# Three sums of softplus: from GpSimd and VectorE instructions to accumulating transfers

## The chip, the cores and the metric

The kernel runs on one core of a Trainium2 chip. The core has five engines with a queue each: PE (TensorE, matrix products), DVE (VectorE), ACT (ScalarE), POOL (GpSimd) and SP (SyncE, which here issues transfers). Sixteen DMA engines move data. Each queue runs in order; queues wait for each other through semaphores. The metric is the device time of one execution in microseconds.

## What is computed

The reference is a two-layer network on images of 8 x 128 x 128 x 96. Layer 0 is a convolution in the frequency domain with a small quantized feed-forward part. Layer 1 is a selective scan in two directions, again with a feed-forward part. The change lies in the step sizes of the scan:

```python
delta = jax.nn.softplus(dts + dt_projs_bias.reshape(1, Kk, DIi, 1))
...
def step(h, inp):
    u, dlt, Bt, Ct = inp
    dA = jnp.exp(dlt[..., None] * As)
    h = dA * h + (dlt * u)[..., None] * Bt[:, :, None, :]
    y = jnp.sum(h * Ct[:, :, None, :], axis=-1)
    return (h, y)
```

The kernel computes softplus(x) as max(x, 0) + log(1 + e), with e = exp(-|x|). Adding 1 to a small e loses low bits, so a correction is kept: with w = 1 + e as rounded, the lost part is (w - 1) - e, and the result is log(w) - ((w - 1) - e) + max(x, 0).

## The kernel before

**Tiles.** `scan_layer` treats two images at a time (four rounds) in chunks of 1,024 tokens: 16 chunks forward (d = 0), then 16 backward (d = 1), 128 in all. The 192 channels of two images make three tiles of 128 rows. A chunk has 12 blocks of 32 channels of one image; a block has 4 units, each with 4 of the 16 states on 128 rows. So a chunk has 48 units, and a unit is one scan.

**A block.** PE spreads `du` (delta times u) over the states (`dub`, `spread`). DVE multiplies it with `bt` for two units at once (`inject`, L1298, 128x2048). ACT makes the decay `da` = exp(delta A) for each unit (`decay`, L1281), with two buffers in PSUM. DVE scans (`scan`, L1333); ACT keeps the last column (`keep`, L1342); POOL multiplies with `ct` (`read`, `hc`, L1349); PE sums over the states (`total`, `y`, L1358). In some blocks of forward chunks (the numbers in `SHARE`) ACT copies `dub` to the SBUF tile `dus` (`fetch`, L1310), and POOL makes the product of the block's last unit (`inject_shared`, L1317), so that DVE's second `inject` has half its size.

**Preparation.** While a chunk is scanned, `prepare_steps` makes delta and `du` of the next one, for three tiles in the order 0, 2, 1. For each: PE's `delta` (`pd`, two halves), ACT's `parts` (|x| into `e`, max(x, 0) into `rl`), ACT's `exp`, `onep` (w = 1 + e) and `log`, DVE's `lost`, POOL's `sub` and `add`, SP's store of w to DRAM (`dld`, from which the scan loads `dlb`), and POOL's `mul` with u (`du`). The tiles `e`, `rl`, `w`, `dus` have one buffer each.

**Beside it.** Forward chunks also carry the depthwise convolution for later chunks (`conv_steps`): nine products on PE for each half tile (`taps`, `pv`, L1081), an eviction on ACT (`evict`, L1095), and after both halves a silu with two loads of ACT's function tables (`silu`, L1106 and L1107). Backward chunks carry output projection and feed-forward part (`finish_steps`) and six gates on POOL (L1414). `pv`, `pd`, `px`, `po` and the feed-forward products share one PSUM buffer, the tag `pp`.

**Order.** It is written out by hand. Every step is given to `plan` with a position in units, and `Plan.emit` issues all steps sorted by it; within an engine that is the order of execution. `PREP` holds the positions of the preparation (relative to the start of the chunk that is being scanned), `SLOTS` those of the convolution: taps from 3.2, 16.2, 26.2, 31.1, 39.1 and 43.6 on, an eviction 4.4 later, the silu 5 after the second.

Of the kernel before, what the change touches and what calls it, by code (L numbers as in the profile page):

```python
# [9 lines left out]
F32 = mybir.dt.float32  # L10
# [3 lines left out]
AF = mybir.ActivationFunctionType  # L14
ALU = mybir.AluOpType
# [14 lines left out]
TC = 1024  # L30
# [911 lines left out]
def scan_layer(tc, p, x2d, xcd, zsd, ud, yfd, dld, bcd, out):  # L942
# [7 lines left out]
    nc = tc.nc  # L950
# [3 lines left out]
    with ExitStack() as ctx:  # L954
# [28 lines left out]
        w1 = ctx.enter_context(tc.tile_pool(name="sc1", bufs=1))  # L983
# [64 lines left out]
        def halves():  # L1048
            return [(i, slice(i * HALF, (i + 1) * HALF)) for i in range(2)]

        def kind(t):
            return 0 if t < 2 else 1
# [74 lines left out]
        def prepare_steps(plan, bp, d, c, k, at0):  # L1127


            k.u, k.du = [None] * 3, [None] * 3  # L1130

            def load(t):
                k.u[t] = w1.tile([128, TC], F32, tag=f"u{t}", name="u")
                nc.sync.dma_start(k.u[t], ud[bp % 2, t, :, c * TC : (c + 1) * TC])

            def project(i, hs):
                def f():
                    if i == 0:
                        k.bc = w1.tile([NX, TC], F32, tag="bc", name="bc")
                    px = ps1.tile([NX, HALF], F32, tag="pp", name="px")  # L1140
                    for t in range(3):
                        nc.tensor.matmul(  # L1142
                            px, xpw[:, d, t, :], k.u[t][:, hs], start=(t == 0), stop=(t == 2)
                        )
                    k.px = px

                return f

            def projected(hs):
                nc.scalar.copy(k.bc[:, hs], k.px)  # L1150

            def store_bc():
                nc.sync.dma_start(bcd[k.s], k.bc[0 : 4 * NST])


            def delta(t, st, i, hs):
                def f():
                    if i == 0:
                        st["e"] = w1.tile([128, TC], F32, tag="e", name="e")
                        st["r"] = w1.tile([128, TC], F32, tag="rl", name="rl")  # L1160
                    pd = ps1.tile([128, HALF], F32, tag="pp", name="pd")
                    nc.tensor.matmul(  # L1162
                        pd, dtw[4 * NST : NX, d, t, :], k.bc[4 * NST : NX, hs], start=True, stop=True
                    )
                    st["pd"] = pd

                return f

            def parts(t, st, hs):
                bias = dtb[:, d, kind(t) : kind(t) + 1]  # L1170
                nc.scalar.activation(st["e"][:, hs], st["pd"], AF.Abs, bias=bias)  # L1171
                nc.scalar.activation(st["r"][:, hs], st["pd"], AF.Relu, bias=bias)  # L1172

            def exp(st):
                nc.scalar.activation(st["e"], st["e"], AF.Exp, scale=-1.0)

            def onep(st):
                st["w"] = w1.tile([128, TC], F32, tag="w", name="w")
                nc.scalar.activation(st["w"], st["e"], AF.Copy, bias=1.0)

            def log(st):
                nc.scalar.activation(st["w"], st["w"], AF.Ln)  # L1182

            def lost(st):
                nc.vector.scalar_tensor_tensor(  # L1185
                    st["e"], st["w"], -1.0, st["e"], ALU.add, ALU.subtract
                )

            def sub(st):
                nc.gpsimd.tensor_tensor(st["w"], st["w"], st["e"], ALU.subtract)  # L1190

            def add(st):
                nc.gpsimd.tensor_tensor(st["w"], st["w"], st["r"], ALU.add)  # L1193

            def store(t, st):
                nc.sync.dma_start(dld[k.s, t], st["w"])

            def mul(t, st):
                k.du[t] = w1.tile([128, TC], F32, tag=f"du{t}", name="du")
                nc.gpsimd.tensor_tensor(k.du[t], st["w"], k.u[t], ALU.mult)  # L1200

            for t, at in ((0, 0.4), (1, 3.2), (2, 4.2)):
                plan(at0 + at, lambda t=t: load(t))
            for i, hs in halves():
                plan(at0 + 9.2 + 1.3 * i, project(i, hs))
                plan(at0 + 10.2 + 1.1 * i, lambda hs=hs: projected(hs))
            plan(at0 + 12, store_bc)
            for t, at in ((0, PREP[0]), (2, PREP[1]), (1, PREP[2])):
                st = {}
                for i, hs in halves():  # L1210
                    plan(at0 + at["delta"][i], delta(t, st, i, hs))
                    plan(at0 + at["delta"][i] + 0.6, lambda t=t, st=st, hs=hs: parts(t, st, hs))
                for what, f in (
                    ("exp", exp), ("onep", onep), ("lost", lost), ("log", log), ("sub", sub),
                    ("add", add),
                ):
                    plan(at0 + at[what], lambda f=f, st=st: f(st))
                plan(at0 + at["mul"], lambda t=t, st=st: mul(t, st))
                plan(at0 + at["store"], lambda t=t, st=st: store(t, st))
# [248 lines left out]
        def finish_steps(plan, bp, c, prs, i, at0, x2_at, at):  # L1468
# [172 lines left out]
            for t, f in zip(at, steps, strict=True):  # L1641
# [7 lines left out]

        PREP = tuple(  # L1650
            {
                "delta": (a0, a1), "exp": e, "onep": e + 0.2, "lost": e + 1.5, "log": e + 2.2,
                "sub": s0, "add": s1, "mul": m, "store": s1 + 1.1,
            }
            for a0, a1, e, s0, s1, m in (
                (12.2, 13.2, 16.2, 20.3, 21.3, 24.3),
                (24.2, 25.2, 28.2, 32.3, 33.3, 36.3),
                (37.2, 38.2, 41.2, 45.3, 48.3, 49.3),
            )
        )  # L1660

        SLOTS = ((3.2, 16.2), (26.2, 31.1), (39.1, 43.6))
# [11 lines left out]
            return [tuple(UN * (n - a) + x for x in s) for a, s in zip(ahead, slots)]  # L1674


        SHARE = (1, 2, 3, 4, 7, 10)
        GATE = (9.9, 17.9, 25.9, 37.3, 41.9, 50.5)

        FINISH = (  # L1680
# [17 lines left out]
        with tc.manual_schedule():  # L1698
            plan = Plan()
            plan(-300, lambda: nc.vector.memset(h0, 0.0))  # L1700
            plan(UN * -2 + 20, prepare_constants)
            plan(UN * -2 + 37, scan_constants)
            for bp in range(B // 2):
                first = len(jobs) * bp
                if bp > 0:
                    plan(UN * (first - 8), lambda: nc.vector.memset(h0[:, 0], 0.0))
                    plan(UN * (first + 8), lambda: nc.vector.memset(h0[:, 1], 0.0))
                for n, (d, c) in enumerate(jobs):
                    k = Params()
                    k.s = n % 4  # L1710
                    at0 = UN * (first + n)
                    share = SHARE if d == 0 and (bp == 0 or n > 0) else ()
                    prs = scan_steps(plan, bp, d, c, k, at0, share)
                    if d == 1:
                        for b2 in range(2):
                            for i in range(2):
                                finish_steps(
                                    plan, bp, c, prs[3 * b2 : 3 * b2 + 3], i, at0, *FINISH[b2][i]
                                )
                    prepare_steps(plan, bp, d, c, k, at0 - UN)  # L1720
                    if d == 0:
                        conv_steps(plan, bp, c, conv_slots(bp, n))
            plan.emit()


@with_exitstack
def kernel(ctx: ExitStack, tc: tile.TileContext, p: Params, out: bass.AP):
    nc = tc.nc
    dp = ctx.enter_context(tc.tile_pool(name="scratch", bufs=1, space=DRAM))
    tall = dp.tile([96, M, 2 * KW], F32, name="tall")  # L1730
    x2d = dp.tile([B, H, W, C + 1], F32, name="x2d")
    xcd = dp.tile([B, M, XROWS, W], F32, name="xcd")
    zsd = dp.tile([B, M, L], F32, name="zsd")
    ud = dp.tile([2, 3, 128, L], F32, name="ud")
    yfd = dp.tile([6, 128, L // 2], F32, name="yfd")
    dld = dp.tile([4, 3, 128, TC], F32, name="dld")
    bcd = dp.tile([4, 4 * NST, TC], F32, name="bcd")

    layer0(tc, p, tall, x2d, xcd, zsd)
    scan_layer(tc, p, x2d, xcd, zsd, ud, yfd, dld, bcd, out)  # L1740
# [109 lines left out]
```

## Time and profile before

| | us |
|---|---|
| median of 3 runs | 26,206.75 (26,201.54 to 26,208.22) |
| profiled execution | 26,211.62 |
| its span, first to last instruction | 26,209.8 |
| DVE busy | 25,009.4 (95%) |
| POOL busy | 22,513.3 (86%) |
| PE busy | 22,077.0 (84%) |
| ACT busy | 17,596.9 (67%) |
| DMA, mean busy share of 16 engines | 41.7% (queue of SP's transfers) |

The profile lists instructions in groups: line, engine, operation, output <- inputs, count, then busy time and the mean length of one, then the idle time of the engine just before them and what ended it. A timeline row gives the start, the length, engine, line and operation of an instruction, or of several of a kind merged (x3), and in brackets the idle time before it. `PEld` is PE's loading of weights, `SPq` the queue of SP's transfers. Layer 0 takes the first 5,100 us or so; the first scan starts at 5,167.47 us, and the 128 chunks follow. The first forward chunks take about 160 us and the first backward ones about 167.

### The profile page before, as it was taken

Reading aid. Unit: us, or ns where it says so; the run is one execution under the profiler, and the core shown is the slowest. Engines: PE = TensorE matmul, PEld = TensorE weight load, DVE = VectorE, ACT = ScalarE, POOL = GpSimd, SP = SyncE. Lnnn points to the kernel's source line nnn. Section 1 sums busy time; section 2 is a strip of 40 time slices with the busy share of each in tenths; the row PEclk is TensorE's granted clock in tenths of the full one; section 3 lists DMA queues with packets and bytes.
Section 4 is the critical chain, followed back from the end, with each engine's and each line's share of the span. In section 5 each row is a group of like instructions: output and inputs, shape, how many; then the busy total and the mean of one; then the engine's idle time right before and its main releaser. Section 6 shows DMA issues by size and latency. Waiting matters only on the chain.

```text
span 26209.8 us, 272243 instructions
## 1 busy us (share of the span) xinstructions
PE 22077.0 (84%) x84560; PEld 8860.1 (34%) x84560; DVE 25009.4 (95%) x18513; ACT 17596.9 (67%) x31774; POOL 22513.3 (86%) x13817
## 2 busy tenths in 40 slices
PE   9999999899997777889877778889777788977777
PEld 7777777522222222222222222222222222212222
DVE  7888888699999999999999999999999999999999
ACT  7888777566666666666666666666666666656666
POOL 5666666499999999999999999999999999999998
PEclk9999999999998888999988889999888899988888
DMA  3333333344444444444444434444444444444443
GB/s 88 93 93 91 90 89 87 106 156 155 153 156 135 138 139 133 156 155 153 154 138 140 136 134 154 157 154 153 139 138 134 138 151 157 156 139 138 136 136 115
DMA packets 1887106, 3513.56 MB, mean 134 GB/s; under 512 B 564382, under 2 KB 999190, under 8 KB 1885626
## 3 DMA queue, kind: packets, MB, share of 16 engines
q1 hardware_dynamic: 1885652, 3496.14, 41.7%
q8 instruction: 672, 11.01, 0.2%
q14 instruction: 782, 6.41, 0.1%
HBM read 2739.32 MB, written 756.17 MB: 133 GB/s over the span
## 4 chain that ended last, share of the span: by engine, by line
DVE 41%; PE 17%; issue 16%; ACT 5%; POOL 3%; DMA 0%; DVEq 0%; POOLq 0%; SPq 0%; ACTq 0%
DVE hp L1333 22%; DVE hp L1298 17%; PE pv L1081 6%; PE y L1358 5%; PE dub L1268 4%; POOL hc L1349 2%; DVE e L1185 2%; ACT da L1281 2%; PE po L1492 1%; PE y L1400 1%; PE px L1142 1%; ACT ff_h L1589 0%; ACT ln_q L1519 0%; PE pd L1162 0%; ACT pre L1095 0%
## 5 line engine op out<-in xcount | busy, mean ns | idle before, releaser
L1349 POOL TENSOR_TENSOR hc<-hp,ct 128x1024 f32<-128x1024 f32 x6144 | 14726.6, 2416 | 1162.7 <-DVE hp L1333 1085.3
L1333 DVE TENSOR_TENSOR_SCAN hp<-da,h,hp 128x1024 f32<-128x1024 f32 x6144 | 14142.8, 2337 | 200.2 <-ACT da L1281 39.6
L1358 PE MATMUL y<-hc,sely 128*32 128x512 f32 x24576 | 6906.9, 646 | 2163.5 <-POOL hc L1349 2145.6
L1281 ACT ACTIVATE da<-dlb,at 128x1024 f32<-128x1024 f32 x6144 | 6845.0, 1114 | 1.1 <-ACT h L1342 1.1
L1298 DVE TENSOR_TENSOR hp<-bt,dub 128x2048 f32<-128x2048 f32 (+1 forms) x3072 | 6551.7, 2133 | 12.7 <-PE dub L1268 12.4
L1268 PE MATMUL dub<-du,selx 128*128 128x512 f32 x6144 | 3686.2, 731 | 1385.5 <-DVE hp L1298 1385.3
L1342 ACT COPY h<-hp 128x1 f32<-128x1 f32 x6144 | 1159.3, 189 | 4831.1 <-DVE hp L1333 4814.5
L1081 PE MATMUL pv<-xin,cdiag 128*128 128x512 f32 x6912 | 3489.9, 624 | 94.2 <-ACT pre L1095 55.1
L1358 PEld LDWEIGHTS y<-hc,sely 128*32 128x32 f32 x24576 | 931.7, 111 | 6682.7 <-POOL hc L1349 4523.0
L1268 PEld LDWEIGHTS dub<-du,selx 128*128 128x128 f32 x6144 | 1237.8, 217 | 3458.5 <-issue 2129.3
L1081 PEld LDWEIGHTS pv<-xin,cdiag 128*128 128x128 f32 x6912 | 1171.9, 190 | 2438.5 <-issue 2035.3
L110 POOL TENSOR_SCALAR ln_v<-ln_v 128x4 f32<-128x4 f32 x768 | 198.7, 259 | 1179.3 <-DVE ln_v L106 1159.2
L1317 POOL TENSOR_TENSOR hp<-bt,dus 128x1024 f32<-128x1024 f32 x366 | 867.2, 2369 | 254.5 <-ACT dus L1310 208.1
L1095 ACT ACTIVATE pre<-pv,cbt 128x512 f32<-128x512 f32 x384 | 263.8, 687 | 1076.4 <-PE pv L1081 889.9
L1190 POOL TENSOR_TENSOR w<-w,e 128x1024 f32<-128x1024 f32 x384 | 903.4, 2353 | 52.0 <-ACT w L1182 38.6
L1162 PE MATMUL pd<-bc,dtw 12*128 12x512 f32 x1536 | 887.5, 658 | 71.7 <-ACT rl L1172 49.3
L111 POOL TENSOR_TENSOR ln_r<-ln_v,mhalf 128x4 f32<-128x4 f32 x768 | 887.1, 1155 | 64.0
L1200 POOL TENSOR_TENSOR du<-w,u 128x1024 f32<-128x1024 f32 x384 | 907.4, 2363 | 0.2
L1193 POOL TENSOR_TENSOR w<-w,rl 128x1024 f32<-128x1024 f32 x384 | 905.3, 2357 | 0.2
L1171 ACT ACTIVATE e<-pd,dtb 128x512 f32<-128x512 f32 x768 | 524.8, 683 | 499.7 <-PE pd L1162 484.6
L770 PE MATMUL ring<-xnt,win 96*128 96x512 f32 x1536 | 778.5, 615 | 69.1 <-ACT xnt L764 68.1
L1142 PE MATMUL px<-u,xpw 128*76 128x512 f32 x1536 | 716.5, 602 | 80.5 <-ACT ff_h L1582 78.3
(189 smaller groups left out, 32830.3 us busy)
## 6 DMA issues: line engine op xcount, KB each, us to landing
dlb<-dld SPq DMA_DIRECT2D x1536, 512.0 KB, 5.3
bt<-bcd SPq DMA_DIRECT2D x1024, 512.0 KB, 5.0
ct<-bcd SPq DMA_DIRECT2D x1024, 512.0 KB, 4.5
u<-ud SPq DMA_DIRECT2D x384, 512.0 KB, 5.0
dld<-w SPq DMA_DIRECT2D x384, 512.0 KB, 3.5
ud<-pre SPq DMA_DIRECT2D x192, 512.0 KB, 3.6
yf<-ud SPq DMA_DIRECT2D x768, 128.0 KB, 4.8
yfd<-yo SPq DMA_DIRECT2D x384, 256.0 KB, 6.5
```

What stands on the lines that cost most here:

```text
L1081: nc.tensor.matmul(st["pv"], cdiag[:, kind(t), j, :], st["xin"][:, r : r + HB // 2, j % 3 : j % 3 + W], start=(j == 0), stop=(j == 8),)
L1142: nc.tensor.matmul(px, xpw[:, d, t, :], k.u[t][:, hs], start=(t == 0), stop=(t == 2))
L1190: nc.gpsimd.tensor_tensor(st["w"], st["w"], st["e"], ALU.subtract)
L1193: nc.gpsimd.tensor_tensor(st["w"], st["w"], st["r"], ALU.add)
L1200: nc.gpsimd.tensor_tensor(k.du[t], st["w"], k.u[t], ALU.mult)
L1268: nc.tensor.matmul(blk["du"][:, hs], selx[:, blk["r"], :], k.du[blk["t"]][:, hs], start=True, stop=True,)
L1281: nc.scalar.activation(un["da"], blk["dl"], AF.Exp, scale=at[:, d, blk["kb"], j : j + 1])
L1298: nc.vector.tensor_tensor(hp[:, 0:n, :], bt[blk["b2"], j][:, 0:n, :], blk["du"].rearrange("p (o t) -> p o t", o=1).to_broadcast([128, n, TC]),
L1333: nc.vector.tensor_tensor_scan(h, da, h, un["init"], op0=ALU.mult, op1=ALU.add)
L1342: nc.scalar.copy(un["init"], un["h"][:, last : last + 1])
L1349: nc.gpsimd.tensor_tensor(un["hc"], un["h"], ct[blk["b2"], j], ALU.mult)
L1358: nc.tensor.matmul(y[q, :], sely, un["hc"][:, hs], start=False, stop=(j == NG - 1),)
```

## The change

`lost` leaves DVE and `sub` and `add` leave POOL's arithmetic. All three become transfers that POOL issues and that add one SBUF tile to another. For that ACT makes m = 1 - w in a new step (`minus`), in the buffer of `dus`. `sub` follows `lost` and `add` by three to four units, the store and `mul` follow `sub` by about three. `add` and `sub` change places. The first tile's `delta` comes a little earlier, the second's a little later. The blocks with shared products are others; their number stays.

```diff
+            def minus(st):
+                st["m"] = w1.tile([128, TC], F32, tag="dus", name="m")
+                nc.scalar.activation(st["m"], st["w"], AF.Copy, scale=-1.0, bias=1.0)
+
             def log(st):
                 nc.scalar.activation(st["w"], st["w"], AF.Ln)
 
+
             def lost(st):
-                nc.vector.scalar_tensor_tensor(
-                    st["e"], st["w"], -1.0, st["e"], ALU.add, ALU.subtract
-                )
+                nc.gpsimd.dma_start(st["e"], st["m"], accum_op=ALU.add)
+
+            def add(st):
+                nc.gpsimd.dma_start(st["w"], st["r"], accum_op=ALU.add)
 
             def sub(st):
-                nc.gpsimd.tensor_tensor(st["w"], st["w"], st["e"], ALU.subtract)
-
-            def add(st):
-                nc.gpsimd.tensor_tensor(st["w"], st["w"], st["r"], ALU.add)
+                nc.gpsimd.dma_start(st["w"], st["e"], accum_op=ALU.add)
...
-                    ("exp", exp), ("onep", onep), ("lost", lost), ("log", log), ("sub", sub),
-                    ("add", add),
+                    ("exp", exp), ("onep", onep), ("minus", minus), ("log", log), ("lost", lost),
+                    ("add", add), ("sub", sub),
...
-                "delta": (a0, a1), "exp": e, "onep": e + 0.2, "lost": e + 1.5, "log": e + 2.2,
-                "sub": s0, "add": s1, "mul": m, "store": s1 + 1.1,
+                "delta": (a, a + 1), "exp": e, "onep": e + 0.2, "minus": e + 1, "log": e + 1.2,
+                "lost": e + 2.1, "add": e + 3.1, "sub": s, "mul": s + 3, "store": s + 2.9,
             }
-            for a0, a1, e, s0, s1, m in (
-                (12.2, 13.2, 16.2, 20.3, 21.3, 24.3),
-                (24.2, 25.2, 28.2, 32.3, 33.3, 36.3),
-                (37.2, 38.2, 41.2, 45.3, 48.3, 49.3),
-            )
+            for a, e, s in ((11.6, 16.2, 22.3), (24.4, 28.2, 34.3), (37.2, 41.2, 47.3))
...
-        SHARE = (1, 2, 3, 4, 7, 10)
+        SHARE = (0, 1, 2, 3, 6, 9)
```

## The prediction, made before the result was known

> **What bounds it now.** I read the busy times first, then the groups of instructions, then DVE's, PE's and ACT's timelines side by side for one chunk. The groups (operation, count, busy us, mean ns, idle before):
>
> ```profile
> L1349 POOL TENSOR_TENSOR hc<-hp,ct 128x1024 f32<-128x1024 f32 x6144 | 14726.6, 2416 | 1162.7 <-DVE hp L1333 1085.3
> L1333 DVE TENSOR_TENSOR_SCAN hp<-da,h,hp 128x1024 f32<-128x1024 f32 x6144 | 14142.8, 2337 | 200.2 <-ACT da L1281 39.6
> ...
> L1185 DVE SCALAR_TENSOR_TENSOR e<-w,e 128x1024 f32<-128x1024 f32 x384 | 535.4, 1394 | 80.7 <-ACT w L1179 80.7
> ```
>
> DVE sets the end: from 8,000 to 11,000 us it is busy 2,971.71 us (99%), POOL 2,789.03 (93%). The 384 corrections of softplus lie in DVE's queue and are 2% of the span. But a forward chunk has a second limit. One of its blocks on DVE (start, length):
>
> ```profile
> 6394.18 2.25 DVE L1298 TENSOR_TENSOR hp<-bt,dub 128x2048 f32<-128x2048 f32 x1
> ...
> 6407.73 2.26 DVE L1298 TENSOR_TENSOR hp<-bt,dub 128x2048 f32<-128x2048 f32 x1
> ...
> 6414.53 6.93 DVE L1333 TENSOR_TENSOR_SCAN hp<-da,h,hp 128x1024 f32<-128x1024 f32 x3
> ```
>
> A plain block takes 13.55 us (6,394.18 to 6,407.73). A block with a shared product takes 12.48 (1.07 less), one correction adds 1.13 to 1.4. PE in the same stretch, from the spread for block 7 to the last convolution tap before block 9, and ACT after it:
>
> ```profile
> 6374.03 3.49 PE L1268 MATMUL dub<-du,selx 128*128 128x512 f32 x4 [1.66 <-DVE hp L1298]
> ...
> 6379.45 1.99 PE L1081 MATMUL pv<-xin,cdiag 128*128 128x512 f32 x4
> ...
> 6408.96 1.13 PE L1081 MATMUL pv<-xin,cdiag 128*128 128x512 f32 x2
> ```
>
> ```profile
> 6410.12 0.69 ACT L1095 ACTIVATE pre<-pv,cbt 128x512 f32<-128x512 f32 x1 [3.31 <-PE pv L1081]
> ...
> 6410.79 1.12 ACT L1281 ACTIVATE da<-dlb,at 128x1024 f32<-128x1024 f32 x1
> 6411.93 1.28 ACT L1106 ACT_TABLE_LOAD   x1
> 6413.22 1.06 ACT L1106 ACTIVATE pre<-pre 128x1024 f32<-128x1024 f32 x1
> 6414.30 1.28 ACT L1107 ACT_TABLE_LOAD   x1
> 6415.59 0.19 ACT L1342 COPY h<-hp 128x1 f32<-128x1 f32 x1
> 6415.69 1.11 ACT L1281 ACTIVATE da<-dlb,at 128x1024 f32<-128x1024 f32 x1
> ```
>
> PE has no idle time for 30.6 us; ACT waits 3.31 us for it, evicts, runs the silu with two table loads, and only then makes the `da` of block 9's third scan, ready at 6,416.80. DVE wants it at about 6,416.7: its three scans take 6.93 us where others take 6.83. The slack of this chain is nought. The same chain ends once more at block 0 of the next chunk (eviction at 6,452.23 after 2.10 us of waiting for PE, `da` ready just before the third scan). So in the second half of a forward chunk PE and ACT are as slow as DVE.
>
> **What the Trainium skill says.** (1) "DMA: Bandwidth & Descriptors", section "SWDGE vs HWDGE vs iDMA": a transfer that accumulates can only be issued from GpSimd, whose cores write its descriptors. Section "Latency and other measured facts" puts the first byte of such a transfer at about 1 us. The trace of before has no transfer from GpSimd. (2) Same page, "Anatomy of one DMA — SWDGE (gpsimd) path": 2.0 us plus bytes at 436 GB/s; for 512 KB an estimate of 3.2 us. (3) "Collectives: The Full Stack", section "The bandwidth ceiling: the fold count and why AG ≠ RS ≠ AR": an add in the DMA path costs two source reads. Nothing here shows that yet. (4) "SBUF — State Buffer", "Who interferes with whom": a DVE instruction with two SBUF inputs and a GpSimd instruction that reads SBUF block each other. The trace agrees: beside a correction (9,132.47) POOL's product takes 3.18 us instead of 2.36, and the correction itself, 1.20 alone, takes up to 2.39. Scans and injections have one input in PSUM and keep their 2.34 and 2.26 us.
>
> **The change, part by part.**
>
> DVE loses 384 corrections. Their pitch is 1394 ns less 80 ns of overlap, 1.31 us: 384 x 1.31 = 503 us. By chunk: forward 1.20 + 1.13 + 1.37 = 3.7 us, reverse 1.14 + 1.14 + 1.92 = 4.2 us; 64 x 7.9 = 506.
>
> POOL loses 768 sums at a pitch of 2.32 us (-1,780 us) and some 0.85 us of blocking per correction. It gains 1,152 DMA issues. Not seen before: at least the 0.33 us that SP's queue needs for the store of `w`, at most what makes POOL the bound. In a reverse chunk POOL has 48 products + 3 `du` at 2.32, four times 3.5 us of finishing steps and six gates of 1.27: 140 us against DVE's 162.6, so nine issues may cost 2.5 us each. I take 1 us (the page): nothing on the path, since DVE and PE are later.
>
> ACT gains 384 `minus`, at the 1.06 us of `onep` (406 us); `log` comes a unit earlier. In a reverse chunk both fit ahead of the next `da` with 0.2 to 1 us left (block 7: ready at +76.3, wanted at +76.5 on the scale of 9,100 us), so I charge 0.4 us a chunk, 0 to 2. In a forward chunk they stand ahead of evictions that wait for PE anyway.
>
> The shared products stay 366, six in a forward chunk: no sum on DVE. But they move from blocks 4, 7, 10 to 0, 6, 9. At 9 and 0 ACT's `fetch` (L1310, 1012 ns, 0.93 in pitch) now stands between the late eviction and the silu, and DVE reaches its third scan 1.07 us sooner.
>
> `delta` of the second tile moves from 24.2/25.2 to 24.4/25.4, so its evictions `parts` (24.8/25.8) fall behind the `da` at 25.0 and 26.0. With T = first scan of block 6: the first parts end at T+4.8 (T+1.9 before), the second `pd` follows, then the spread (3.3 us), the pair's opening and a sum: convolution starts at T+11.3 where it was T+10.1.
>
> The sums are now a chain: two transfers, `sub` three units behind, store and `mul` three more. POOL waits at `sub` and `mul`, with the products of later units queued behind, whose readers are PE's sums and DVE's buffers; three units are 9 to 11 us. ACT waits for `sub` before `parts` at 25.0 rewrites `e`. From POOL's place in the trace `sub` goes out about 3 us before T and `parts` wants `e` at T+3.5: 6.5 us. Nearest rows: the store of `w` lands in 3.5 us, loads in 5.3; by the pages 3.2 us plus a second read 1.2, plus queueing. Bounds 3.5 and 12; I take 6, which just fits; the range keeps both ends. The transfers put 604 MB more on engines that are 41.7% busy with 3,496 MB: +7 to +15%.
>
> SP's store moves from 22.4 to 25.2 (and 34.4 to 37.2, 49.4 to 50.2) and waits for `sub`; behind it are loads of `dlb` issued seven units ahead, the store's own reader comes 15 units later. `u` of tile 1 waits for `mul` at 50.3 and has six units until its projection. Both nothing. `dus` now also holds `m`: the lost transfer has five units to release it. Nothing. The first chunk, before DVE works, changes by +-10 us.
>
> **The sum.** Forward chunk with full convolution (59 of 64): from third scan of block 0 to T 71.7 us (71.9 before: lost correction -1.13, block 4 no longer shared +1.07). From T to the third scan of block 9: 11.3 + 30.6 (PE) + 0.59 + 1.15 + 0.93 + 3.66 + 1.25 = 49.5, where it was 10.1 + 30.6 + 6.7 = 47.4. From there to the third scan of the next block 0: 41.1 before (PE again has no idle time), +0.75 with the fetch: 41.85. Together 163.05 against 160.35: +2.7 us, although DVE has less to do. 59 x 2.7 = +159. The five others, with little or no convolution, save 3 us each. Reverse: 64 x (-4.2 + 0.4) = -243. Sum -99 us. The profiled execution took 26,211.6 us (span 26,209.8); the median of the runs, 26,206.75, is 4.9 below. Predicted: 26,107 us.
>
> **Rivals.** (B) The chains have slack that I don't see, or PE's 3.49 us spread shrinks to 1.9 (most others take 1.88): convolution then starts at T+9.7, a forward chunk costs +1.1, -200 us in all: 26,007; with everything hidden -506: 25,700. For it: DVE's 99%. Against: the 6.93 us and PE without gaps. (C) Slower: the transfers land late. Each us beyond 6.5 between `sub` and `parts` at 25.0 delays the convolution, and with it `da`, one for one in 59 chunks; above 9.7 us the reverse chunks too. -99 + 59 x (t - 6.5) is zero at 8.2 us. At 10.5: +236 + 50 - 99, 26,395 us; at 12 some +400. For it: two reads, a software issue, engines already half busy. Against: 3.5 us for a store of that size. (D) An issue holds POOL for over 2.5 us and POOL becomes the bound: at 3.5 us a reverse chunk takes 140 + 31.5 = 171.5 us (167.2 now), a forward one, with 57 products and 31.5, 164 (160.3 now): +510, about 26,720. For it: descriptors written by software; against: the page's 1 us. (E) The transfers don't happen as said: excluded, they are nine DMA issues in POOL's queue per chunk.
>
> **Numbers.** My case 0.45 (own range 26,000 to 26,250), B 0.15, C 0.27, D 0.10, cancelling 0.03. A measurement tells about 0.2% (52 us) from no change. Faster: 0.32 + 0.15 = 0.47; same 0.16; slower 0.37. The range, with C's upper part and B's lower, is 25,860 to 26,520.
>
> **What would show it.** No L1185 row; DVE idle before scans 400 us higher, most `<-ACT da`, in forward chunks at blocks 8, 9 and 0; reverse chunks near 163 us, forward ones near 163; POOL under 90%; accumulating transfers landing in 5 to 8 us. Wrong if forward chunks shorten by over 2 us (B), if `parts` waits for DMA (C), or if POOL's gaps vanish (D).

## The result, and the profile after

The changed kernel takes 26,572.8 us (median of 4 runs, 26,567.8 to 26,597.3) against 26,206.5 (4 runs) for the kernel before on the same chip: ratio 1.0142, 95% interval 1.0124 to 1.0160. It is 1.4% slower; 26,107 us was predicted.

Chunk times, read from the starts of DVE's scans, say where it went (means over all chunks):

| | forward chunk | backward chunk | span |
|---|---|---|---|
| before | 160.78 us | 167.22 us | 26,209.8 us |
| after | 167.41 us | 166.09 us | 26,566.0 us |

64 x 6.63 = +424 us in forward chunks, 64 x 1.13 = -72 us in backward ones: +352 of the 356 us between the spans. DVE does less (24,568.1 us busy, 25,009.4 before) and waits more. The groups of the page after:

```profile
L1352 POOL TENSOR_TENSOR hc<-hp,ct 128x1024 f32<-128x1024 f32 x6144 | 14794.6, 2456 | 2056.7 <-DVE hp L1336 1842.2
L1336 DVE TENSOR_TENSOR_SCAN hp<-da,h,hp 128x1024 f32<-128x1024 f32 x6144 | 14132.2, 2337 | 566.9 <-ACT da L1284 411.9
...
L1301 DVE TENSOR_TENSOR hp<-bt,dub 128x2048 f32<-128x2048 f32 (+1 forms) x3072 | 6565.9, 2137 | 526.5 <-ACT dus L1313 288.9
```

Lines have moved by three: `inject` is L1301, `fetch` L1313, `scan` L1336. The row of DVE's corrections is gone. The waits of scans for `da` went from 39.6 to 411.9 us, as foreseen. Not foreseen is the last row: DVE's products wait 288.9 us for `dus`, the copy of the spread product that ACT makes for shared blocks. In the trace of before, what waited for that copy and what waits now (tile, engine and line, us, times; before first):

```profile
  POOL hp L1317: 208.1, 187
```

```profile
  DVE hp L1301: 288.9, 178
  POOL hp L1320: 259.7, 123
```

Before, DVE never waited for the copy. One place where it does now, block 0 of a forward chunk, DVE and then ACT:

```profile
6173.96 2.35 DVE L1336 TENSOR_TENSOR_SCAN hp<-da,h,hp 128x1024 f32<-128x1024 f32 x1
6179.17 1.22 DVE L1301 TENSOR_TENSOR hp<-bt,dub 128x1024 f32<-128x1024 f32 x1 [2.86 <-ACT dus L1313]
6180.31 2.34 DVE L1336 TENSOR_TENSOR_SCAN hp<-da,h,hp 128x1024 f32<-128x1024 f32 x1
6184.01 4.59 DVE L1336 TENSOR_TENSOR_SCAN hp<-da,h,hp 128x1024 f32<-128x1024 f32 x2 [1.35 <-ACT da L1284]
```

```profile
6177.50 0.69 ACT L1095 ACTIVATE pre<-pv,cbt 128x512 f32<-128x512 f32 x1 [4.57 <-PE pv L1081]
6178.08 1.00 ACT L1313 COPY dus<-dub 128x1024 f32<-128x1024 f32 x1
6179.10 1.28 ACT L1106 ACT_TABLE_LOAD   x1
...
6182.86 1.11 ACT L1284 ACTIVATE da<-dlb,at 128x1024 f32<-128x1024 f32 x1
```

Read the two together. ACT's queue holds the eviction of the convolution (planned at 48.0) ahead of the copy (48.1). The eviction waits 4.57 us for PE's last tap; the copy ends at 6,179.08, and DVE's half product starts 0.09 us later. The silu follows, and the `da` of the third scan is ready at 6,183.97, so DVE waits once more. Over the steady forward chunks (the fourth to the fourteenth of each round) DVE loses 2.97 + 1.35 us at block 0 in this way, 1.31 + 1.33 at block 9, 0.70 at block 2.

The delay also goes back to PE, which may not write the next spread into `dub` before the half product has read it. At block 9, DVE and then PE:

```profile
6135.05 1.22 DVE L1301 TENSOR_TENSOR hp<-bt,dub 128x1024 f32<-128x1024 f32 x1 [1.31 <-ACT dus L1313]
```

```profile
6136.32 2.69 PE L1271 MATMUL dub<-du,selx 128*128 128x512 f32 x4 [1.25 <-DVE hp L1301]
```

In a steady block 9 PE is idle for 3.8 us, against 2.1 before.

That both engines read `dub` makes them take turns. The Trainium skill, "PSUM — Partial Sum Buffer", section "PSUM bank collisions raise a hardware error", says that the compiler orders instructions of different engines that touch one bank in the same quarter of its partitions, reads as well as writes. The program agrees: each of the 366 half products waits for a semaphore of ACT, before as after, and none of the 2,706 full ones does. And the trace agrees, with the 0.09 us.

PE's stretch from the second half of a forward chunk, which the prediction showed for before:

```profile
6093.73 2.07 PE L1162 MATMUL pd<-bc,dtw 12*128 12x512 f32 x2 [0.28 <-ACT rl L1172]
6095.73 3.78 PE L1271 MATMUL dub<-du,selx 128*128 128x512 f32 x4
...
6101.55 1.98 PE L1081 MATMUL pv<-xin,cdiag 128*128 128x512 f32 x4
...
6112.06 1.88 PE L1271 MATMUL dub<-du,selx 128*128 128x512 f32 x4
...
6131.05 1.13 PE L1081 MATMUL pv<-xin,cdiag 128*128 128x512 f32 x2
```

T, the first scan of block 6, is 6,088.68 here: convolution starts at T+12.9 and takes the same 30.6 us as before. And the transfers (queue, count, size, median us from issue to landing):

```profile
e<-m POOLq DMA_DIRECT2D x384, 512.0 KB, 5.3
w<-rl POOLq DMA_DIRECT2D x384, 512.0 KB, 9.8
w<-e POOLq DMA_DIRECT2D x384, 512.0 KB, 7.4
```

### The profile page after: what moved, and what is told of

Its sections match the earlier page's. It is cut to its first block, busy times and chain, and to the rows that moved or that the text cites. A ratio compares the mean times of both kernels' runs of the same rounds, so it can differ in the third digit from the quotient of the medians.

```text
span 26566.0 us, 273309 instructions
## 1 busy us (share of the span) xinstructions
PE 22843.8 (86%) x84560; PEld 9088.0 (34%) x84560; DVE 24568.1 (92%) x18129; ACT 17918.0 (67%) x32158; POOL 21446.5 (81%) x14201
## 3 DMA queue, kind: packets, MB, share of 16 engines
q0 software_dynamic: 165888, 604.05, 12.3%
## 5 line engine op out<-in xcount | busy, mean ns | idle before, releaser
L1336 DVE TENSOR_TENSOR_SCAN hp<-da,h,hp 128x1024 f32<-128x1024 f32 x6144 | 14132.2, 2337 | 566.9 <-ACT da L1284 411.9
L1361 PE MATMUL y<-hc,sely 128*32 128x512 f32 x24576 | 7222.9, 677 | 2403.2 <-POOL hc L1352 2396.5
L1301 DVE TENSOR_TENSOR hp<-bt,dub 128x2048 f32<-128x2048 f32 (+1 forms) x3072 | 6565.9, 2137 | 526.5 <-ACT dus L1313 288.9
L1271 PE MATMUL dub<-du,selx 128*128 128x512 f32 x6144 | 3852.9, 760 | 450.5 <-DVE hp L1301 447.4
L1271 PEld LDWEIGHTS dub<-du,selx 128*128 128x128 f32 x6144 | 1342.2, 236 | 2810.0 <-issue 2087.4
L1162 PE MATMUL pd<-bc,dtw 12*128 12x512 f32 x1536 | 1130.2, 823 | 156.6 <-ACT rl L1172 153.5
L1585 ACT CAST ff_h<-ph 128x512 f16<-128x512 f32 x768 | 441.9, 575 | 387.9 <-PE ph L1572 386.0
L1417 POOL TENSOR_TENSOR yo<-yo,zs 128x512 f32<-128x512 f32 x384 | 499.4, 1300 | 237.1 <-ACT yo L1410 236.2
```

Of the source, the lines that this page charges most:

```text
L1162: nc.tensor.matmul(pd, dtw[4 * NST : NX, d, t, :], k.bc[4 * NST : NX, hs], start=True, stop=True)
L1271: nc.tensor.matmul(blk["du"][:, hs], selx[:, blk["r"], :], k.du[blk["t"]][:, hs], start=True, stop=True,)
L1301: nc.vector.tensor_tensor(hp[:, 0:n, :], bt[blk["b2"], j][:, 0:n, :], blk["du"].rearrange("p (o t) -> p o t", o=1).to_broadcast([128, n, TC]),
L1336: nc.vector.tensor_tensor_scan(h, da, h, un["init"], op0=ALU.mult, op1=ALU.add)
L1361: nc.tensor.matmul(y[q, :], sely, un["hc"][:, hs], start=False, stop=(j == NG - 1),)
```

## The experiments

**Which theory.** P: the place of the shared products makes the loss. T: the transfers make it (traffic, issues, landings). All ratios are against the kernel before on the same chip, with 95% intervals. "Base" is the changed kernel with old sharing and old `delta` places (`e4_both`).

| run | us | ratio | forward, backward chunk |
|---|---|---|---|
| e1_old_share | 26,272.1 | 1.0024 (1.0014 to 1.0033) | 162.80, 166.38 |
| e2_before_new_share | 26,573.4 | 1.0137 (1.0122 to 1.0152) | 166.32, 167.29 |
| e3_old_delta | 26,577.9 | 1.0141 (1.0124 to 1.0158) | 167.57, 166.20 |
| e4_both (base) | 26,219.9 | 1.0003 (0.9995 to 1.0012) | 162.02, 166.05 |
| f5_no_minus | 26,110.6 | 0.9960 (0.9945 to 0.9975) | 161.99, 164.39 |
| f6_no_transfers | 26,019.7 | 0.9926 (0.9911 to 0.9941) | 160.43, 164.55 |
| f7_neither | 25,974.5 | 0.9908 (0.9894 to 0.9923) | 160.37, 163.89 |
| f8_small | 26,036.5 | 0.9934 (0.9917 to 0.9950) | 160.62, 164.52 |
| h1_early_fetch | 26,341.4 | 1.0051 (1.0034 to 1.0068) | 164.07, 165.66 |
| g1_sub_early | 26,041.9 | 0.9936 (0.9921 to 0.9950) | 160.50, 164.67 |
| g3_lost_only | 26,183.2 | 0.9989 (0.9983 to 0.9996) | 160.45, 166.97 |
| k1_silu_late | 26,037.9 | 0.9933 (0.9916 to 0.9950) | 160.50, 164.76 |
| i1_after_sub_early | 26,463.0 | 1.0097 (1.0082 to 1.0112) | 166.82, 164.79 |
| i2_after_sub_early_old_delta | 26,445.1 | 1.0091 (1.0074 to 1.0108) | 166.54, 164.85 |

**Sharing put back in the changed kernel, and put into the kernel before.**

```diff
-        SHARE = (0, 1, 2, 3, 6, 9)
+        SHARE = (1, 2, 3, 4, 7, 10)
```

> The kernel after, with the shared products back at blocks 1, 2, 3, 4, 7, 10 of a forward chunk. Theory P (place): a forward chunk grew from 160.4 to 167.9 us because blocks 0 and 9 need ACT's copy of the spread product just when ACT is behind the convolution's late evictions, and DVE's second product of such a block waits for that copy; the transfers are not to blame. It then falls by the waits at blocks 0 and 9 (some 5 us) to about 163, T to the third scan of block 9 stays near 50.5 us because convolution still starts 12.9 us after T: about 26,270 us. Theory T (transfers: their traffic, or the issues on POOL, slow PE and the loads): the place hardly matters, 26,500 to 26,570.

The reverse edit in the kernel before, without a transfer:

> The kernel before, with the shared products at blocks 0, 1, 2, 3, 6, 9 and nothing else changed: no transfers. Theory P: DVE's second product waits for the copy at blocks 0 and 9 here as well, a forward chunk takes 163.5 to 165 us instead of 160.4, about 26,430 us (26,390 to 26,490). Theory T: within 50 us of the kernel before.

26,272 and 26,573 us. The place alone, with no transfer in the program, costs 362 us (26,573.4 less 26,211.2, the median of before in that series), as much as the whole change; undoing it in the changed kernel brings 301 us. Theory P holds, and more strongly than I had put it for the second run. DVE's waits for the copy in that run (waiter, releaser, us, times, longest):

```profile
DVE hp L1298 <- ACT dus L1310: 203.2, 122, 3.1
```

They lie in part elsewhere than I had said: 1.5 us a steady chunk at block 0, 1.8 at block 2, which both kernels share, and only 0.1 at block 9. To these come 1.35 and 0.84 us of waiting for `da` at blocks 0 and 9.

**The copy moved ahead of the eviction**, sharing as changed:

```diff
-                        plan(gb + 0.1, fetch(blk))
+                        plan(gb - 1.3, fetch(blk))
```

> The kernel after, sharing at 0, 1, 2, 3, 6, 9 and all else as it is, only ACT's copy of the spread product planned 1.4 units earlier (at -1.3 units of its block instead of +0.1), ahead of the late eviction. Theory P (DVE's second product of a shared block waits for the copy, and the copy for the eviction): DVE's waits for dus at blocks 0, 9 and 2 (5 us a forward chunk) go, forward chunks 163 to 164, 26,270 to 26,350 us. Rival (one more ACT pass in PE's stretch costs wherever it stands, or the two blocks are simply dear): 26,480 or more.

26,341 us, 232 less, with the six blocks where the change put them. What waits for the copy in this run:

```profile
  DVE hp L1301: 100.8, 1
```

178 waits have become one (the first product of all, at the start of layer 1). It is the order of copy and eviction in ACT's queue that makes most of the cost (232 of the 301 us that old sharing brings), not the choice of blocks as such. 69 us more than with old sharing remain: here the third scans of blocks 0 and 9 wait 2.7 and 1.8 us for `da`, with old sharing 1.0 and 0.7. That the copy in ACT's queue does this is likely, but not tested.

**`delta` put back**, alone and with the sharing:

```diff
-            for a, e, s in ((11.6, 16.2, 22.3), (24.4, 28.2, 34.3), (37.2, 41.2, 47.3))
+            for a, e, s in ((11.6, 16.2, 22.3), (24.2, 28.2, 34.3), (37.2, 41.2, 47.3))
```

> The kernel after, with the second tile's delta product back at 24.2 and 25.2 units (it is at 24.4 and 25.4), sharing as in the kernel after. Theory P: convolution starts 10.3 to 11 us after T instead of 12.9, the waits for da at blocks 8, 9 and 0 shrink by some 2 us a forward chunk, 26,430 us. Theory T: 26,520 to 26,570.

> The kernel after, with both undone: sharing at 1, 2, 3, 4, 7, 10 and delta at 24.2 and 25.2; the transfers, ACT's minus and the rest of the order stay. Theory P: forward chunks near 160.5 us (PE's stretch is then as in the kernel before), reverse chunks stay at 166.2: about 26,090 us, faster than before. Theory T: 26,400 or more, forward chunks above 165 us.

Alone it brings nothing (26,578), against my expectation; with old sharing 52 us. The base equals the kernel before within 0.1%, where I had expected 26,090: something still takes back what DVE and POOL were relieved of. In the base `parts` of the second tile starts 0.1 us (median) after the landing of `sub` in 64 of 64 forward chunks, and so it does in `e3_old_delta`, after waiting 3.0 us for it: the landing has taken the place of the later `delta`. One such place in the base, POOL's issue and ACT's wait:

```profile
6376.82 0.87 POOL L1196 DMA_DIRECT2D w<-e  x1
```

```profile
6384.97 0.69 ACT L1171 ACTIVATE e<-pd,dtb 128x512 f32<-128x512 f32 x1 [3.70 <-DMA w<-e]
```

8.15 us lie between them. `parts` may not rewrite `e` while `sub` still reads it.

**What takes the gain back: ACT's pass, the traffic, or the landing.** Four kernels on the base: `minus` left out (the first transfer adds `r`), the transfers left out, both left out, and the transfers cut to 64 of 1,024 columns:

```diff
-                nc.gpsimd.dma_start(st["w"], st["e"], accum_op=ALU.add)
+                nc.gpsimd.dma_start(st["w"][:, 0:64], st["e"][:, 0:64], accum_op=ALU.add)
```

> Base: the kernel after with old sharing and old delta places (26,220 us; forward chunks 162.0, reverse 166.05; DVE still loses 6.4 and 4.2 us a chunk to waits). Here ACT's pass minus is left out, and the first transfer adds r instead of m; all three transfers and their places stay (log moves with nothing else). It leaves out 1 - w of the correction. Theory A (ACT: minus and the earlier log stand ahead of da): waits for da at reverse blocks 6, 7 and forward blocks 5, 8, 0 shrink, 1 to 2 us a chunk, 26,000 to 26,100 us. Theory T (traffic or issues of the transfers): 26,180 to 26,230.

> Same base, with minus kept and the three transfers left out with their issues (the three sums of softplus are left out, so softplus is the log alone). Theory A: 26,150 to 26,220, waits for da as in the base. Theory T: the waits go, reverse chunks near 163.5, forward near 160: 25,900 to 26,000.

> Same base, with the three transfers and minus both left out (softplus is the log alone): DVE and POOL lose the sums for nothing. It bounds what can be had from taking the sums off DVE and POOL in this order of work. By DVE's count alone 3.7 and 4.2 us a chunk under before: 25,700; if PE's stretch from the start of convolution to its last eviction (30.7 us) sets forward chunks, those stay at 159.5 to 160.5 and only reverse ones fall to 163: about 25,920.

> Same base, all three transfers kept in their places but over 64 of 1,024 columns (38 MB instead of 604 MB; the sums of the other columns are left out). If traffic is what costs: as with no transfers at all. If POOL's issues and the waits for landings cost: as the base, 26,200.

Both theories have a part, and each run fell 10 to 20 us outside the range of the theory that it speaks for. Without `minus` 109 us go, nearly all in backward chunks. Without transfers 200 us go, with small ones 183: POOL's 1,152 issues cost next to nothing (17 us apart), size does. The two don't add up: without either, 25,974 us, 245 less and not 309. That is all that the relief of DVE and POOL can bring in this order, 0.4 us in a forward chunk and 3.3 in a backward one.

Size could act through traffic or through the time to land. So full transfers, issued earlier:

```diff
-                "lost": e + 2.1, "add": e + 3.1, "sub": s, "mul": s + 3, "store": s + 2.9,
+                "lost": e + 2.1, "add": e + 2.2, "sub": s - 1, "mul": s + 3, "store": s + 2.9,
```

> The kernel after with old sharing and old delta places (26,220 us), with the second transfer a unit earlier (beside the first) and the third a unit earlier. Theory C (the third transfer lands 8.1 us after its issue, and parts of the second tile, which rewrites e, starts 0.1 us after that landing in 64 of 64 forward chunks, so convolution starts at T+11.9): the wait goes, convolution starts near T+10.5, forward chunks 160.5 to 161 as with small transfers: about 26,110 us. Rival (traffic slows the loads and PE in general): 26,190 to 26,230.

26,042 us: issued earlier, full transfers cost no more than small ones (26,036) and 22 us more than none (26,020), which is within the intervals. In forward chunks that is the chain as expected: convolution starts at T+10.4 (T+11.9 in the base). `sub` takes as long as ever where it counts (8.3 us median), but who waited for it, in the base and then here:

```profile
  ACT e L1171: 202.4, 56
```

```profile
  ACT e L1171: 11.6, 11
```

POOL, too, now waits for `add` ahead of `sub` (240.6 us in 136 times), and that doesn't show in the chunk times. Backward chunks gain 1.4 us, which I hadn't expected. In the base `parts` starts right at the landing in only 17 of 63 of them, so what makes this gain is not shown. This kernel beats both: 0.64% faster than before, 2.0% faster than the changed one (26,041.9 against 26,572.8, from two series).

**Two tries to go further.** Only the correction as a transfer, POOL's sums kept:

```diff
-                "delta": (a0, a1), "exp": e, "onep": e + 0.2, "lost": e + 1.5, "log": e + 2.2,
+                "delta": (a0, a1), "exp": e, "onep": e + 0.2, "minus": e + 1.0, "lost": e + 1.9, "log": e + 2.2,
```

> The kernel before, its sharing, places and POOL's two sums kept; only DVE's correction is replaced, by ACT's minus and one accumulating transfer (201 MB). If the sum is right that the runs give (neither minus nor transfers 25,974; minus +45; a third of what full transfers cost over small ones, +60): 26,080 us, faster than before. If POOL's sums back in its queue cost what the relief of DVE brings: 26,180 or more.

26,183 us, the rival's number: backward chunks stay at 166.97, DVE waiting for `da` and `dub`. This suggests that POOL's relief counts there, not DVE's alone; no run takes it apart from the other differences in the order. And the silu behind the third `da`, on the best kernel:

```diff
-                plan(begin[1] + 5, silu(t, st))
+                plan(begin[1] + 5.95, silu(t, st))
```

> The best kernel so far (old sharing, old delta places, second transfer beside the first, third a unit earlier: 26,042 us, forward chunks 160.4) with the convolution's silu planned 0.95 units later, behind the da of the third scan at blocks 9 and 0 instead of ahead of it. Theory S (what is left in a forward chunk is the chain late eviction, silu with two table loads, da of the third scan): waits for da at blocks 9 and 0 (1.4 us) go, forward chunks 159 us, about 25,960 us. Rival (PE's stretch alone sets the chunk: a scan that starts sooner meets the next matmul as late): 26,020 to 26,060.

No difference, 160.50 us again, but the edit didn't take the wait away. DVE at block 9, in `g1_sub_early` and then here:

```profile
6583.16 4.63 DVE L1336 TENSOR_TENSOR_SCAN hp<-da,h,hp 128x1024 f32<-128x1024 f32 x2 [0.75 <-ACT da L1284]
```

```profile
6574.35 4.58 DVE L1336 TENSOR_TENSOR_SCAN hp<-da,h,hp 128x1024 f32<-128x1024 f32 x2
6579.72 2.35 DVE L1336 TENSOR_TENSOR_SCAN hp<-da,h,hp 128x1024 f32<-128x1024 f32 x1 [0.79 <-ACT da L1284]
```

The third scan no longer waits, but the fourth does: its `da` now stands behind the silu. The waits at blocks 9 and 0 are 1.4 us a steady chunk as before (and the one at block 5 went over to block 8). So neither theory S nor its rival is settled. Six kernels (f6, f7, f8, g1, g3, k1) have forward chunks of 160.4 to 160.6 us, with DVE idle for some 5 us of a steady chunk and PE for 14 to 16, less than 1 us of it in any of blocks 1, 7, 8, 10 and 11. Which wait fixes the number stays open.

**Does the landing cost in the changed kernel itself?** The earlier transfers with the changed sharing, then with old `delta` places as well:

> The kernel after, sharing and delta places as they are, with the second transfer beside the first and the third a unit earlier. If landing and sharing cost apart from each other, the landing is out of the way here but delta at 24.4 still puts parts behind the da at 25: forward chunks 1 to 2 us shorter, reverse ones 1 us: about 26,430 us. If the wait for the copy at blocks 0 and 9 covers the landing: only the reverse chunks gain, 26,510.

> The same with delta of the second tile at 24.2 and 25.2 as well; what is left of the change against the kernel before is then the sharing, minus and the transfers out of the way. If costs add: the kernel before with the new sharing (26,573) less what the best kernel gains over before (168): 26,400, forward chunks 166.5 and reverse 164.7. If the wait covers it: 26,510.

110 and 128 us less than the changed kernel, in each case between the two numbers expected. Backward chunks gain 1.2 to 1.3 us, nearly what they gained on the base. Forward ones gain 0.6 us with `delta` late and 1.0 with `delta` early in both (167.57 to 166.54), where the base gained 1.5: the costs add in part, and later `delta` and the wait for the copy cover the rest of the landing. What is left in a forward chunk (166.5 to 166.8) is where the place of sharing alone had put the kernel before (166.32).

## Why the prediction was wrong, step by step

**Shared products: the step that failed.** I charged ACT's copy 0.93 us in the chain eviction, silu, `da`, and counted DVE's third scan 1.07 us sooner. I left out that DVE's half product waits for the copy, so that a copy late in ACT's queue stops DVE at once. The term for this wait was nothing. From the third scan of block 9 to that of the next block 0 I worked out 41.85 us; it took 44.43. I had PE without idle time there, but its spread had to wait for the late half product. With sharing alone moved the stretch took 44.43 too (41.07 before), and the one from block 0 to T grew from 71.6 to 74.5. In sum the place of sharing cost 5.5 us a forward chunk there, 355 us, and 4.6 in the changed kernel. The view that would have told was there: the list of those who wait for the copy, and ACT's order at 35.5/36.1 and 48.0/48.1 units, an eviction waiting for PE right ahead of the copy in each case.

**`delta` later.** I had convolution start at T+11.3; it started at T+12.9, and from T to the third scan of block 9 took 51.2 us, not 49.5 (47.7 before). The 1.2 us that I charged for the place itself were nearly right with old sharing (T+12.9 in e1, T+11.9 in e4). The first `parts` end at T+5.1, close to the 4.8 that I had. What is missing comes after them: PE runs at half rate, so that the second `pd` takes 2.07 us (1.24 before) and the spread 3.76 (3.3 charged), 1.3 of the missing 1.6 us. With landing and `delta` both out of the way (i2) convolution still starts at T+12.2, against T+10.4 with old sharing (g1); sharing alone in the kernel before has T+9.0. So the place of sharing acts here only together with the new order, and how is not shown.

**Landing.** Taken as 6 us, within a budget of 6.5; measured 8.1 where it counts (7.4 over all). C's mechanism is real in forward chunks: 178 us lie between base and `g1_sub_early`, 1.5 us a forward and 1.4 a backward chunk. C's sum crosses zero at 8.2 us, and the base is indeed level with the kernel before, but that is luck in part: C let backward chunks lose only from 9.7 us on. In the changed kernel `parts` starts within 0.3 us of the landing in 60 of 64 forward chunks too, but ACT waits only 15.5 us for `sub` in all, because the later `delta` brings it there at nearly the same time (`parts` starts at T+3.8; I had T+3.5).

**`minus`.** Charged 0.4 us a backward chunk (26 us); measured 1.66 (109 us in all) in the base, and 0.66 (45 us) where no transfer was in the way. The term was too small by two to four times. It fell where I had 0.2 us left: the `da` of block 7 comes 1.3 us late with `minus` (f6), 0.2 without (f7).

**DVE's relief.** 503 us were on DVE, and I held that forward chunks couldn't use them because PE and ACT are as slow. The outcome was right: 160.37 us without corrections and without anything in their place, 160.78 with them. There (f7) DVE is idle for 5.1 us of a steady chunk (1.6 before), 3.5 of them waiting for `da` at blocks 8, 0 and 9. That fits the reason that I gave, but which chain holds the chunk stays open. Backward chunks gave 3.3 us of 4.2.

**POOL.** Right: an issue took 0.87 to 1.2 us, POOL is busy 81%, and rival D is out. That the 1 us taken fits is luck in part: the page gives it for the first byte, not for POOL's own time. SP's store (4.4 us to land, 3.5 before) and the first scan (5,165.4 us, 5,167.5 before) cost nothing, as said. The transfers take 12.3% of the DMA engines' time, within 7 to 15%, and that load alone costs nothing measurable (g1 against f6).

**The sum.** Forward +144 us predicted (+159 and the five others), +424 measured; backward -243 predicted, -72 measured. (By the terms shown, the stretch before T comes to 71.84 us, not 71.7, which adds 8 us.) The first error is mostly the copy. The second is 2.7 us a chunk: `minus` and the transfers together cost 2.16 (base against f7) where I charged 0.4, and the relief was worth 0.9 less than the count.

## What to carry to other kernels

When a step is moved in a hand-written order, look up who waits for its result and what stands ahead of it in its own queue: a 1 us copy behind an eviction that waits for PE cost more than all that the change saved. A transfer that replaces an engine's instruction has a landing time in its price, and the step that rewrites its source buffer pays it; issued early enough, 604 MB cost next to nothing here. Before paying for the relief of a busy engine, leave the work out in one run: here that showed 0.9% as the most that could be had.

## What the hardware showed beyond that

- Accumulating transfers of 512 KB between SBUF tiles took 5.3, 9.8 and 7.4 us (medians) to land in one kernel, by their place in the order. The third alone took 8.1, 5.0 and 8.9 us for the three tiles of a forward chunk. With all three cut to 32 KB it took 4.2 (f8), so more than half of its time isn't its bytes.
- PE's rate after idling: four products of a spread took 3.78 us at 6,095.73 and 1.88 at 6,112.06 above. The Trainium skill, "TensorE: Matmul & The Clock Gate", section "What's actually happening", has the clock at half after at least one idle window of about 3.4 us, and at full after at least one busy one. The trace agrees on the two rates: it records a granted clock of 0.5 from 6,086.26 to 6,099.91 us and 1.0 after that. If an idle window is one without any work, the trace doesn't agree on that. PE's gaps around that turn were 1.7 and 2.2 us long. At the 194 turns to half in the steady forward chunks of the changed kernel, and in the 5 us before each, none was longer than 2.23, and in the median PE was busy for half of the 3.4 us before. Nor did one busy window bring it back: that stretch lasted 13.65 us, and PE was idle for hardly any of it after 6,087.68.
- So a stall can lengthen what comes after it. PE is at half rate for 31 us of a steady forward chunk after and for 12 before, and busy for 151.9 and 144.7 us, with the same work; the best kernel has 14 and 144.8. Alone this doesn't set the time: with sharing moved in the kernel before (e2) it is 17 us, and the run takes as long as the changed kernel.
